# A phase seam in a fused adapter kernel: the last two layer norms finished on VectorE, and the first x of the next phase turned six pairs early

## The chip, the cores and the metric

The kernel runs on one core of a Trainium2 chip. Its engines are TensorE (PE in the profile, PEld for its weight loads), VectorE (DVE), ScalarE (ACT), GpSimd (POOL) and SyncE (SP, which here issues nearly all DMAs). The metric is the device time of one execution in microseconds, as the median of several executions. Before the change it is 3129.63 us (three runs, 3129.15 to 3130.18).

## The reference

The input x has 128 samples of 128 rows and 1024 columns (H), in float32. Each sample has a role from 0 to 2, which picks its weights. Two layers of the same form follow one another:

```python
def _L0_cond_ref(role, hidden_states, W_down, b_down, W_up, b_up, gamma, beta):
    h = jnp.einsum('bsh,bhk->bsk', hidden_states, W_down[role]) + b_down[role][:, None, :]
    h = jax.nn.gelu(h, approximate=False)
    u = jnp.einsum('bsk,bkh->bsh', h, W_up[role]) + b_up[role][:, None, :]
    y = hidden_states + u
    mean = jnp.mean(y, axis=-1, keepdims=True)
    var = jnp.mean(jnp.square(y - mean), axis=-1, keepdims=True)
    yn = (y - mean) * jax.lax.rsqrt(var + LN_EPS)
    return yn * gamma[role][:, None, :] + beta[role][:, None, :]
```

K, the width in between, is 512. The second layer takes the first one's output and its own weights.

## The kernel before

The work has four phases: down of layer 0, up of layer 0, down of layer 1, up of layer 1. Each phase goes over 64 items: 63 pairs of samples with the same role, and one pair of left-over samples (place 31 of the order). Pair n is item n in the first half and item n + 1 behind the left-overs, so the last two items of a phase are the pairs 61 and 62. Between the phases the data goes through DRAM: `hd` holds the hidden values, `mid` the output of layer 0.

A pair is one matrix product of 2 x 2 blocks done with seven block products instead of eight (the Winograd form). `item_products` gives them as steps s1 to s7 at the times 0, 2, 4 ... 12, and an item starts every 7 slots, so that the steps of two neighbouring items alternate on PE. The seven weight blocks have the names B11, B21, T2, T1, T3, B22, T4. They lie in `wall`, which has eight slots: seven for the phase at work and a spare one, into which the next phase's B11 is loaded early. Each block has three places, one for each role; the first 21 pairs of a phase use place 0 alone.

The seven products need sums of blocks of the transposed input. `Down.load` and `load_rest` bring x in eight quarter loads (L404), `turn` (L546) transposes one sample on VectorE, and `winograd_sums` (L413) makes four additions on POOL (L418 to L421). For the first three items of the second down phase there is no free buffer for x, so it goes into parts of weight blocks that aren't loaded yet (`among_weights`): item 0 into places 1 and 2 of B11, which lies in the slot that was spare.

In an up phase VectorE adds each product to x (L681, L690). At the end of a pair (`Up.finish`) each sample goes through: `squares` on ACT, ending in a power on POOL (L794); `scaled` on VectorE (L801); `stored`, for sample 0 a multiplication on ACT (L808) and an addition of beta on POOL (L809), for sample 1 one operation on VectorE (L811); `away`, the store to `mid` (L815).

What sets the order is a list of events with times in slots (`at`). The program runs through them in order of time and ties each instruction to the one before it on its engine. So every engine, and SP's queue of DMAs, works strictly in the order of the event times, however late it is. The loads of a phase's weight blocks (L937) and of the next x stand in the same SP queue as the stores of `away`. The event times of item 0 of phase 2, relative to its start, are: load -15, first turn with the rest of `prepare` -6.9, second turn and sums -3.5.

Of the kernel before, what the change touches and what calls it, by code (L numbers as in the profile page):

```python
# [14 lines left out]
ENG = mybir.EngineType  # L15
# [4 lines left out]
P = 128  # L20
SQ = 32
NQ = P // SQ
# [4 lines left out]
def kernel(  # L27
# [36 lines left out]
    ORDER = ["B11", "B21", "T2", "T1", "T3", "B22", "T4"]  # L64
# [8 lines left out]
    NI = NPAIR + 1  # L73
# [99 lines left out]
    class Sums:  # L173
# [23 lines left out]
        def load(self, q):  # L197
            if q == 0:
                self.role = reg(role_of, self.k, [ENG.SP], R - 1)
            rows = self.w.shape[1] // NQ  # L200
            src = self.w[ds(self.role, 1), ds(q * rows, rows), :]
            nc.sync.dma_start(self.whole[ts(q, SQ)], src.rearrange(self.rows, i=SQ))
# [196 lines left out]
    def quartered(t, srcs):  # L399

        for s, src in enumerate(srcs):
            n = src.shape[-1] // NQ
            for q in range(NQ):
                nc.sync.dma_start(  # L404
                    t[s][ts(q, SQ)], src[:, ts(q, n)].rearrange("(a t) c -> t a c", t=SQ)
                )
# [110 lines left out]
    class Down:  # L517
# [5 lines left out]
            self.tag = f"d{layer}_{n}"  # L523

        def load(self):
            if self.among_weights:


                block = self.ph.weights[ORDER[self.m]].v
                self.xq = [block[:, 1 + s] for s in range(2)]  # L530
            else:
                self.xq = [flat("q", 4, f"xq{self.tag}_{s}", H) for s in range(2)]
            self.xq = [t.rearrange("p (a c) -> p a c", a=NQ) for t in self.xq]
            if self.early:
                quartered(self.xq[0:1], [self.early_x(0, ENG.SP)])
                return
            self.srcs = x_of(self.layer, self.n, ENG.SP)
            quartered(self.xq[0:1], self.srcs[0:1])

        def load_rest(self):  # L540
            quartered(self.xq[1:2], [self.early_x(1, ENG.SP)] if self.early else self.srcs[1:2])

        def early_x(self, s, engine):
# [14 lines left out]
                self.turn(0)  # L558

        def prepare(self):  # L560
            self.begin_turns()
            self.sums = None
            set_places(self, [ENG.PE, ENG.Activation])
            if not self.early and self.n < NPAIR:
                self.sums = flat("s", 3, "S" + self.tag, 1792)[:, 0:1536].rearrange(
                    "p (m j c) -> p m j c", m=3, c=P
                )

        def end_turns(self):
            if self.early:  # L570
                return
            self.turn(1)
            if self.n < NPAIR:
                winograd_sums(self.sums, self.a, nc.vector if self.ph is phases[0] and self.m == 1 else nc.gpsimd)

# [47 lines left out]
    class Up:  # L623
# [150 lines left out]
        def finish(self):  # L774
            if self.last:
                return self.finish_last()
            steps = []
            for s in range(2):
                t = (10.4, 12.4)[s] if self.n < NPAIR else (10.9, 12.65)[s]
                one = lambda n: small.tile([P, 2], F32, tag=n, name=n + self.tag, bufs=6)  # L780
                box = {}
                row = lambda t, s=s: self.row(t, s)
                if self.before_last and s == 1:
                    before_last[:] = [self, box]

                def squares(s=s, box=box, one=one):
                    part, box["m"], box["v"] = one("part"), one("mean"), one("var")
                    nc.scalar.mul(part, self.stat[:, s], -1.0 / H)  # L788
                    m, v = box["m"][:, 0:1], box["v"][:, 0:1]
                    nc.scalar.activation(m, part[:, 0:1], AF.Identity, bias=part[:, 1:2])  # L790
                    box["o"] = flat("q", 4, f"o{self.tag}_{s}", H)
                    nc.scalar.activation(box["o"], self.x[:, s], AF.Square, bias=m, accum_out=v)  # L792
                    nc.scalar.activation(v, v, AF.Identity, bias=eps, scale=1.0 / H)  # L793
                    nc.gpsimd.tensor_tensor(v, v, mhalf[:, 0:1], ALU.pow)  # L794

                def scaled(s=s, box=box, row=row):
                    if self.before_last and s == 1:
                        nc.scalar.activation(box["o"], self.x[:, s], AF.Identity, bias=box["m"][:, 0:1])
                        nc.gpsimd.tensor_tensor(box["o"], box["o"], row(self.ph.gamma), ALU.mult)
                        return  # L800
                    nc.vector.scalar_tensor_tensor(  # L801
                        box["o"], self.x[:, s], box["m"][:, 0:1], row(self.ph.gamma), ALU.add, ALU.mult
                    )

                def stored(s=s, box=box, row=row):
                    o, v = box["o"], box["v"][:, 0:1]
                    if s == 0 and not self.before_last:
                        nc.scalar.mul(o, o, v)  # L808
                        nc.gpsimd.tensor_tensor(o, o, row(self.ph.beta), ALU.add)  # L809
                    else:  # L810
                        nc.vector.scalar_tensor_tensor(o, o, v, row(self.ph.beta), ALU.mult, ALU.add)  # L811

                def away(s=s, box=box):
                    if self.layer == 0:
                        nc.sync.dma_start(mid[self.n][s], box["o"])  # L815
                    else:
                        i = reg(perm, 2 * self.n + s, [ENG.SP], B - 1)
                        result(i, box["o"], slice(0, H), nc.sync)

                steps += [(t, squares), (t + 1.3, scaled)]  # L820


                if not (self.before_last and s == 1):
                    steps.append((t + (3.2 if self.before_last else 3.1), stored))
                    steps.append((t + (5.4, 4.2)[s], away))
            return steps
# [4 lines left out]
    SLOTS = 7  # L831
# [3 lines left out]
    def at(time, step):  # L835
        heapq.heappush(events, (time, next(count_), step))
# [7 lines left out]
    for k, ph in enumerate(phases):  # L844
        for m, n in enumerate(sequence):
            base = SLOTS * (k * NI + m)
            box = {}
            kind = Up if ph.up else Down

            def load(box=box, ph=ph, n=n, kind=kind, m=m):  # L850
                item = box["item"] = kind(ph, n)
                item.m = m
                item.early = ph is phases[0] and m == 0
                item.last = ph is phases[-1] and m == NI - 1
                item.before_last = ph is phases[-1] and m == NI - 2
                item.among_weights = ph is phases[2] and m < 3
                if m == left_over_at + 1:
                    item.SEED = -1.65
                item.load()


            if ph.up:
                first, rest = (-16 if m < 3 else -11.5), -7
            elif k == 0:
                first = {0: -30, 1: -19, 2: -19, 3: -17.4}.get(m, -19)
                rest = -28 if m == 0 else first + 0.05
            else:
                first = -15 if m == 0 else -11.9
                rest = first + 0.1
            at(base + first, load)  # L870
            at(base + rest, lambda box=box: box["item"].load_rest())

            def go(box=box, base=base):
                item = box["item"]
                item.prepare()
                if not item.among_weights:
                    item.end_turns()
                for time, step in item.products() + item.finish():
                    at(base + time, step)


            prepare = {1: 4.5 - base, 2: 8.6 - base}.get(m, kind.PREPARE) if k == 0 else kind.PREPARE
            if ph is phases[2] and m < 3:

                prepare = -6.9
                at(base - 3.5, lambda box=box: box["item"].end_turns())
            at(base + prepare, go)
        if k + 1 < len(phases):

# [43 lines left out]
            for name, (slot, free) in zip(ORDER, places):  # L933
                nxt.weights[name] = block = Block(slot)

                def load_part(k, to=block, src=scratch[nxt.layer, nxt.up][name]):
                    nc.sync.dma_start(to.v[:, k], src[:, k])  # L937


                at(base + free + 0.75, lambda f=load_part: f(0))  # L940
                for k_ in range(1, R):
                    later_on = SLOTS * (1 + 2 * ORDER.index(name) + k_)
                    at(base + later_on - 2.75, lambda f=load_part, k_=k_: f(k_))
    for i, job in enumerate(later):
        start = SLOTS * (7 + 6 * i)
# [72 lines left out]
```

## Time and profile before

| what | us |
|---|---|
| median of three runs | 3129.63 |
| the profiled execution | 3130.06 |
| its span, first to last instruction | 3128.3 |
| PE busy | 3112.7 |
| VectorE busy | 1975.8 |
| POOL busy | 1777.3 |
| ACT busy | 1203.5 |
| share of the 16 DMA engines (main queue) | 66.2% |

The page gives busy time by engine, the waits that ended last before an instruction, and a timeline in which each row has a start, a length, the engine, the line of the kernel and the tiles (out, then in). `xTd` is a transposed x, `Sd` the sums, `bd`, `ad` and `ed` are PSUM banks of a down item, `bu`, `au` and `eu` those of an up item, `ou` is an output on its way to the store, `varu` its variance. A row's bracket tells how long the engine stood before it and what released it. PE is busy in 99% of the span, with its clock at 0.999 of full speed on average. Around 1560.6 us the second down phase starts; this place is called the seam here.

### The profile page before, as it was taken

To read this page: it belongs to the slowest core of one execution; us is meant where nothing else is said; L and a number is where in the kernel's file an instruction comes from. 1 tells how busy PE (TensorE), PEld (TensorE's weight loads), DVE (VectorE), ACT (ScalarE), POOL (GpSimd) and SP (SyncE) were. 2 spreads that over 40 slices of the span, in tenths; PEclk is the share of its full clock that TensorE was granted. 3 is DMA by queue.
4 is the path that set the end of the run, shared out by engine and by line. 5 is a ranking of instruction groups with operands and counts; after the bars stand their busy time and mean duration, and the time that the engine had idled before them with its cause. 6 is when DMAs were issued, how large, how long until landed. Compare 5 with 4: busy or idle time off the path is not lost.

```text
span 3128.3 us, 42229 instructions
## 1 busy us (share of the span) xinstructions
PE 3112.7 (99%) x10796; PEld 2047.8 (65%) x10796; DVE 1975.8 (63%) x2807; ACT 1203.5 (38%) x2816; POOL 1777.3 (57%) x1391
## 2 busy tenths in 40 slices
PE   9999999999999999999999999999999999999999
PEld 6888888888544444444478888888884444444443
DVE  6554544544678777777864444444447877777777
ACT  1222222222454555454432222222224545454544
POOL 3545344444577767777654343444436777677775
PEclk9999999999999999999999999999999999999999
DMA  8778788876786565656687555555567765656564
GB/s 218 196 216 209 212 206 210 213 209 196 272 288 240 211 227 208 225 212 226 225 224 179 146 130 131 130 127 138 126 183 275 280 239 206 227 207 226 211 227 176
DMA packets 429735, 642.21 MB, mean 205 GB/s; under 512 B 35778, under 2 KB 305603, under 8 KB 428356
## 3 DMA queue, kind: packets, MB, share of 16 engines
q1 hardware_dynamic: 428930, 637.15, 66.2%
q8 instruction: 102, 1.67, 0.2%
q10 hardware_dynamic: 578, 2.36, 0.2%
q14 instruction: 125, 1.02, 0.1%
HBM read 405.02 MB, written 234.36 MB: 204 GB/s over the span
## 4 chain that ended last, share of the span: by engine, by line
PE 49%; POOL 1%; issue 0%; DMA 0%; SPq 0%; DVE 0%; ACT 0%; DVEq 0%; POOLq 0%; ACTq 0%
PE bu L427 14%; PE bd L427 14%; PE eu L427 7%; PE ed L427 7%; PE au L427 3%; PE ad L427 3%; POOL ou L809 0%; SPq L404 0%; DMA hd<-hd 0%; POOL Sd L420 0%; POOL Sd L418 0%; DMA wall<-mid 0%; POOL varu L794 0%; POOL xTd L419 0%; DVE ou L712 0%
## 5 line engine op out<-in xcount | busy, mean ns | idle before, releaser
L427 PE MATMUL bu<-wall,hTu 128*128 (+1 forms) x2048 | 921.3, 592 | 0.0
L547 DVE STREAM_TRANSPOSE xTd<-xqd 128x1024 f32<-128x1024 f32 (+1 forms) x252 | 504.9, 2071 | 350.7 <-PE bd L427 283.8
L427 PEld LDWEIGHTS bu<-wall,hTu 128*128 128x128 f32 x2048 | 389.1, 190 | 487.2 <-issue 456.6
L418 POOL TENSOR_TENSOR Sd<-xTd 128x512 f32<-128x512 f32 x124 | 159.7, 1288 | 790.4 <-DVE xTd L547 782.7
L794 POOL TENSOR_TENSOR varu<-varu,mhalf 128x1 f32<-128x1 f32 x254 | 329.6, 1298 | 393.8 <-ACT varu L793 393.8
L427 PE MATMUL bd<-wall,xTd 128*128 (+1 forms) x2064 | 487.1, 379 | 1.8 <-ACT bd L445 1.8
L427 PE MATMUL eu<-wall,hTu 128*128 (+1 forms) x1040 | 488.0, 592 | 0.0
L427 PE MATMUL bd<-wall,Sd 128*128 (+1 forms) x2000 | 472.8, 379 | 2.2 <-ACT hd L606 1.6
L427 PEld LDWEIGHTS bd<-wall,xTd 128*128 128x128 f32 x2064 | 392.0, 190 | 57.5 <-ACT bd L445 2.6
L427 PEld LDWEIGHTS bd<-wall,Sd 128*128 128x128 f32 x2000 | 379.7, 190 | 56.5 <-issue 2.6
L801 DVE SCALAR_TENSOR_TENSOR ou<-xu,meanu,tables 128x1024 f32<-128x1024 f32 x253 | 325.3, 1286 | 138.3 <-ACT ou L792 120.0
L611 ACT ACTIVATE hd<-hd 128x256 f32<-128x256 f32 x379 | 157.6, 416 | 534.5 <-DVE hd L610 534.4
L427 PEld LDWEIGHTS eu<-wall,hTu 128*128 128x128 f32 x1040 | 197.6, 190 | 247.4 <-issue 218.8
L788 ACT ACTIVATE partu<-statu 128x2 f32<-128x2 f32 x254 | 51.6, 203 | 728.7 <-DVE xu L690 728.7
L809 POOL TENSOR_TENSOR ou<-ou,tables 128x1024 f32<-128x1024 f32 x126 | 296.9, 2356 | 0.0
L792 ACT ACTIVATE ou<-xu,meanu 128x1024 f32<-128x1024 f32 x254 | 291.7, 1148 | 8.4
L681 DVE TENSOR_TENSOR xu<-bu,xu 128x512 f32<-128x512 f32 x256 | 176.1, 688 | 119.1 <-PE bu L427 119.1
L427 PE MATMUL ed<-wall,xTd 128*128 (+1 forms) x1064 | 251.0, 379 | 0.0
L418 POOL TENSOR_TENSOR hTu<-hTu 128x256 f32<-128x256 f32 x126 | 198.1, 1572 | 70.8 <-DVE hTu L656 49.0
L427 PE MATMUL au<-wall,hTu 128*128 (+1 forms) x504 | 236.8, 592 | 0.0
L427 PE MATMUL ed<-wall,Sd 128*128 (+1 forms) x1000 | 236.3, 379 | 0.1
L427 PE MATMUL ad<-wall,xTd 128*128 (+1 forms) x1000 | 236.2, 379 | 0.0
(135 smaller groups left out, 3383.1 us busy)
## 6 DMA issues: line engine op xcount, KB each, us to landing
xqd<-in_x_dram SPq DMA_DIRECT2D x512, 128.0 KB, 3.3
hd<-hd SPq DMA_DIRECT2D x256, 256.0 KB, 2.4
xu<-in_x_dram SPq DMA_DIRECT2D x128, 512.0 KB, 3.8
mid<-ou SPq DMA_DIRECT2D x128, 512.0 KB, 4.2
xu<-mid SPq DMA_DIRECT2D x128, 512.0 KB, 3.8
out_dram<-ou SPq DMA_DIRECT2D x125, 512.0 KB, 3.8
hqu<-hd SPq DMA_DIRECT2D x244, 256.0 KB, 5.0
xqd<-mid SPq DMA_DIRECT2D x488, 128.0 KB, 3.8
```

The costliest lines, as they stand in the source:

```text
L418: engine.tensor_tensor(dst[:, 1], a11, a21, ALU.subtract)
L427: nc.tensor.matmul(ps[:, 0:cols], a[:, j], w.rhs(r, j, cols), start=start and j == 0, stop=j == n - 1, skip_group_check=True,)
L547: nc.vector.transpose(self.a[:, s, chunks].rearrange("p j (t a) -> p j a t", t=SQ), self.xq[s].rearrange("p a (i j) -> p j a i", i=SQ)[:, ...
L611: nc.scalar.activation(y, y, AF.Gelu)
L681: nc.vector.tensor_tensor(y, ps, y, ALU.add)
L788: nc.scalar.mul(part, self.stat[:, s], -1.0 / H)
L792: nc.scalar.activation(box["o"], self.x[:, s], AF.Square, bias=m, accum_out=v)
L794: nc.gpsimd.tensor_tensor(v, v, mhalf[:, 0:1], ALU.pow)
L801: nc.vector.scalar_tensor_tensor(box["o"], self.x[:, s], box["m"][:, 0:1], row(self.ph.gamma), ALU.add, ALU.mult)
L809: nc.gpsimd.tensor_tensor(o, o, row(self.ph.beta), ALU.add)
```

## The change

Three things are changed.

- The last two pairs of the first up phase (`ending`) finish sample 0 as sample 1 is finished, in one operation on VectorE; both samples' last operation and store get earlier event times (2.5 and 3.6 behind the squares, in place of 3.1 and 4.2 or 5.4).
- Item 0 of the second down phase (`ahead`) gets its x much earlier. Both samples are loaded one after the other into place 0 of B11's block in the spare slot (events at -42 and -31.5), and turned (-34.8 and -24.3) into places 1 and 2 of the same block, from which PE reads them. The sums move from -3.5 to -8.4. Item 0 has no buffer of its own for the transposed x any more.
- Since B11's places 1 and 2 hold x until item 0 is done, the loads of places 1 and 2 for the second down phase change their turn: B21 comes first, B11 last.

```diff
         def load(self):
+            if self.ahead:
+                self.srcs = x_of(self.layer, self.n, ENG.SP)
+                self.a = self.ph.weights[ORDER[0]].v[:, 1:3].rearrange("p s (j c) -> p s j c", c=P)
+                return
             if self.among_weights:
...
+        def load_ahead(self, s):
+
+            self.xq = [self.ph.weights[ORDER[0]].v[:, 0].rearrange("p (a c) -> p a c", a=NQ)] * 2
+            quartered(self.xq[s : s + 1], self.srcs[s : s + 1])
+
         def load_rest(self):
+            if self.ahead:
+                return
             quartered(self.xq[1:2], [self.early_x(1, ENG.SP)] if self.early else self.srcs[1:2])
...
         def prepare(self):
-            self.begin_turns()
+            if not self.ahead:
+                self.begin_turns()
...
-            self.turn(1)
+            if not self.ahead:
+                self.turn(1)
...
+            ending = self.layer == 0 and self.m >= NI - 2
...
-                    if s == 0 and not self.before_last:
+                    if s == 0 and not self.before_last and not ending:
                         nc.scalar.mul(o, o, v)
                         nc.gpsimd.tensor_tensor(o, o, row(self.ph.beta), ALU.add)
                     else:
...
                 steps += [(t, squares), (t + 1.3, scaled)]
+                if ending:
+                    steps += [(t + 2.5, stored), (t + 3.6, away)]
+                    continue
...
+                item.ahead = ph is phases[2] and m == 0
...
+            elif m == 0:
+                first = rest = -43
+                for s in range(2):
+                    at(base - 42 + 10.5 * s, lambda box=box, s=s: box["item"].load_ahead(s))
+                    at(base - 34.8 + 10.5 * s, lambda box=box, s=s: box["item"].turn(s))
             else:
-                first = -15 if m == 0 else -11.9
+                first = -11.9
                 rest = first + 0.1
...
-                prepare = -6.9
-                at(base - 3.5, lambda box=box: box["item"].end_turns())
+                prepare = -6.9 if m else -8.5
+                at(base - 3.5 if m else base - 8.4, lambda box=box: box["item"].end_turns())
...
                 for k_ in range(1, R):
-                    later_on = SLOTS * (1 + 2 * ORDER.index(name) + k_)
+
+                    turn = ORDER.index(name) if nxt.up else (ORDER.index(name) - 1) % len(ORDER)
+                    later_on = SLOTS * (1 + 2 * turn + k_)
                     at(base + later_on - 2.75, lambda f=load_part, k_=k_: f(k_))
```

## The prediction

> **What bounds the kernel.** I read the page's busy table first, then the waits of PE, then busy time in slices of 10 us around the seam between the first up phase and the second down phase, then the timeline of that seam engine by engine, and last the slices in which PE's clock is not full.
>
> ```profile
> span 3128.3 us, 42229 instructions
> ...
> PE 3112.7 (99%) x10796; PEld 2047.8 (65%) x10796; DVE 1975.8 (63%) x2807; ACT 1203.5 (38%) x2816; POOL 1777.3 (57%) x1391
> ```
>
> PE is idle for 15.6 us in all. Nothing else bounds the kernel, so an edit is worth what it does to PE's waits. About 11.5 us of the idle time lie in the first 40 us and the last 12 us, which the change doesn't touch. The rest lies at the seam (columns: stretch, its length, then busy us of PE, PEld, DVE, ACT, POOL, PE clock, DMA share, GB/s):
>
> ```profile
> 1560.00:1570.00 10.00, 9.51 (x35) 6.22 (x34) 8.35 (x11) 4.83 (x11) 8.43 (x7) 1.00 0.94 321
> 1570.00:1580.00 10.00, 9.10 (x37) 6.45 (x35) 8.13 (x9) 5.03 (x14) 5.64 (x4) 1.00 0.79 209
> 1580.00:1590.00 10.00, 8.53 (x37) 6.77 (x37) 9.33 (x7) 4.04 (x11) 6.39 (x5) 1.00 0.55 197
> 1590.00:1600.00 10.00, 8.74 (x41) 7.38 (x41) 5.43 (x6) 2.35 (x7) 7.66 (x6) 1.00 1.06 291
> ```
>
> PE misses 0.49, 0.90, 1.47 and 1.26 us: 4.1. Ends of matmuls are modelled, so I count starts: from the product that starts at 1560.62 (first of the down phase) to the one at 1599.30 there are 19 steps in 38.68 us, at an even pace of 1.725 (the chain has 3.45 for two products) 32.78. **5.9 us are lost at the seam, and that is all the change can win: 0.19%.** The bound for a measured difference is 0.2%, 6.26 us.
>
> The first wait is for the weight block T2, and its queue tells why it is late:
>
> ```profile
> 1552.58 1.32 POOL L794 TENSOR_TENSOR varu<-varu,mhalf 128x1 f32<-128x1 f32 x1 [2.45 <-ACT varu L793]
> ...
> 1553.87 2.38 POOL L809 TENSOR_TENSOR ou<-ou,tables 128x1024 f32<-128x1024 f32 x1
> ...
> 1556.28 0.32 SPq L815 DMA_DIRECT2D mid<-ou  x1
> 1556.65 5.07 SPq L404 DMA_DIRECT2D wall<-mid  x8
> ...
> 1562.30 2.03 SPq L937 DMA_DIRECT2D wall<-T  x3
> ...
> 1568.16 1.97 PE L427 MATMUL bd<-wall,Sd 128*128 128x256 f32 x8 [0.49 <-DMA wall<-T]
> ```
>
> SP issues in order. It stood 5.4 us (waits of the queue) for POOL's beta addition of pair 60, sample 0 (ends 1556.27), then issued that store, eight quarters of x for item 1, another store, and only then T2: 6.02 us after POOL's end. PE got T2 5.86 us after its issue. PE wanted it at 1565.79 + 1.725 = 1567.52.
>
> **The change, part by part.**
>
> *The turns of item 0.* Two transposes leave the seam (2.0 us each: the row at 1554.01 is followed at 1556.02) and go into the up phase, one into each of the pairs that start some 57 and 45 us before the seam: the new order puts the first behind the addition at 1503.30, the second behind the one at 1521.93.
>
> ```profile
> 1503.30 0.69 DVE L681 TENSOR_TENSOR xu<-bu,xu 128x512 f32<-128x512 f32 x1
> ...
> 1521.93 0.68 DVE L690 SCALAR_TENSOR_TENSOR xu<-eu,xu 128x512 f32<-128x512 f32 x1
> ...
> 1533.90 0.68 DVE L690 SCALAR_TENSOR_TENSOR xu<-eu,xu 128x512 f32<-128x512 f32 x1
> ```
>
> The first runs 1503.91 to 1505.92; the addition behind it started at 1504.17: VectorE is 1.75 late. Does it catch up? From 1521.93 to 1533.90 VectorE and ACT, already late, need 11.97 for a pair, PE 12.01 (products at 1512.56 and 1524.57). So late stays late. The second turn adds 0.67: behind it VectorE waited 1.27 for ACT in any case (1521.93 + 0.62 + 2.01 + 0.61 = 1525.17, where the scaling started at 1524.50). Sum **+2.4 us** on all that follows in the up phase; bounds 0 (caught up) and 4.0 (both in full). PE feels a little of it: the third product of pair 59 is drained at 1526.3 + 0.7 = 1527.0 instead of 1523.2, and the next product on that bank was due at 1526.28: about 0.8, and 0.4 more in the next pair. I don't add these 1.2, since the wait below ends later whatever PE lost before.
>
> *Their eight x loads* go from 1534.8 (one batch of 4.7 us on SP) to two batches of four among pairs 56 to 58. SP issues 2.9 us per up pair there, so I cost them at nothing; if that cover were gone, a load of x for a pair would be 2.4 us late, against about 4 us it has in hand.
>
> *The sums of item 0 on POOL.* Four additions, in the new order behind the power of pair 60, sample 1, and **ahead of the beta addition of pair 60, sample 0**, on which SP waits. The power ended at 1553.90; with +2.4 it ends at 1556.3. The sums take 5.3 us undisturbed (1606.43 to 1611.74). They are disturbed: POOL and VectorE exclude one another on such operations.
>
> ```profile
> 1569.61 2.34 POOL L809 TENSOR_TENSOR ou<-ou,tables 128x1024 f32<-128x1024 f32 x1
> 1569.67 3.36 DVE L811 SCALAR_TENSOR_TENSOR ou<-ou,varu,tables 128x1024 f32<-128x1024 f32 x1 [0.34 <-POOL varu L794]
> ```
>
> The later starter stands until the other is done (1571.95) and then needs 1.08. Two VectorE operations (L811 of pair 60, L801 of pair 61) fall into the sums' time and cost POOL about 1.05 each: first sum to 1557.6, L811 to 1558.6, second sum 1559.8, third 1561.1, fourth 1562.5, L801 to 1563.5, and the beta addition (2.2 behind a collision) to **1565.8** where it was 1556.27. Bounds: 1561.7 (no lateness, no collision: 1553.9 + 5.4 + 2.4) and 1567.4 (4.0 late).
>
> *What is queued behind it.* On SP: the store, eight quarters of item 1, a store, T2, T1, T3, B22. T2 is issued 6.0 later, at 1571.8 (1570.9 if the batch takes 4.15, as at 1572.35), and lands 5.86 later by its own row, 3.65 at the least (B21 at 1550.52 on quiet engines, by its landing in the trace). I take 1571.4 + 5.6 = **1577.0** for PE's start; ends 1574.5 and 1579.2. On POOL: the power of pair 61, sample 0, for which VectorE's new L811 of that sample now waits (to 1566.4), and behind that the drain of pair 62's e bank, which PE needs at 1567: a new wait of 1 to 2 us on PE. It lies inside the wait for T2.
>
> *PE's clock.* PE then stands idle for some 7 us at once.
>
> ```profile
> 15.00:16.00 1.00, 0.98 (x2) 0.49 (x3) 1.00 (x2) 0.00 (x0) 0.00 (x0) 0.85 1.05 265
> 16.00:18.00 2.00, 2.00 (x4) 0.70 (x3) 1.97 (x2) 0.00 (x0) 0.00 (x0) 0.50 1.05 249
> ...
> 3122.50:3125.00 2.50, 0.16 (x1) 0.00 (x0) 1.42 (x2) 0.58 (x1) 0.00 (x0) 1.00 0.70 287
> 3125.00:3126.00 1.00, 0.00 (x0) 0.00 (x0) 0.00 (x0) 0.00 (x0) 0.00 (x0) 0.62 1.02 397
> ```
>
> The last column but two is the granted clock. It halves 2.6 us after PE's last matmul (3122.66, clock 0.62 over 3125 to 3126), and after the thin start of the kernel PE works at half clock from 15.7 to 19.1 (the stretch of 18 to 19 has 0.50 too, that of 19 to 20 has 0.94): 3.4 us that did 1.7 us of work. Waits of up to 1.5 us at the seam left it at 1.00. I add **1.75**; ends 0 (the clock stays) and 3.5 (twice that stretch). [...]
>
> *The end on VectorE.* For sample 0 of pairs 61 and 62 ACT's multiplication (1.13) and POOL's addition (2.35) go and VectorE gets L811 (1.27): 2.5 more on VectorE. In return both L811 of sample 1 lose their collision (3.36 to 1.27): 4.2 less, besides the two turns. The stores of 61 no longer wait on POOL for 7 us. So the five later waits (three for ACT, which stood behind VectorE; one for POOL's sums; one for an h buffer whose store was behind SP's wait) have less reason, and PE comes 9 us later to them. I cost them at nothing. The nearest is the h store: SP gets there at about 1595, it lands 5.2 later, and PE asks at 1591.7 + 11.3 = 1603.
>
> *The loads of places 1 and 2* of each block move by one turn (B21 first, B11 last): as many loads at the same times. Their first use is at pair 21, the last now lands at pair 13. Nothing.
>
> **Sum.** 1577.0 - 1567.5 = 9.5, refill 0.1, clock 1.75: 11.3 lost at the seam in place of 5.9: **+5.4 us**. On the profiled execution (3130.06, span plus 1.76) that is 3135.5; on the median 3129.63, which is 0.43 less, **3135.0**: +0.17%, within the bound.
>
> **Rivals.** *T2 later still (slower).* In the old run T2 left SP ahead of the crowd. Now T2, T1, T3, B22 and the next batch go out without a pause, and the old rows of T1 to B22 show 6.5 to 7.4 us to landing. With 7.4 behind 1571.8 PE starts at 1579.2: 11.7 + 0.1 + 1.75 - 5.9 = +7.6, 3137.2. It decides from a start at 1577.9. Against it: T2 is still the first of that crowd.
>
> *The waits go.* If the sums cost the store nothing (POOL stands idle 2.4 us before each power), only T2's own 0.7 stays of the 5.9: -5.2, 3124.4. For it: VectorE loses 4 us of work at the seam. Against it: the order on POOL is fixed, the sums behind that power and ahead of that addition.
>
> [...]
>
> **How the numbers follow.** Forecast 0.50 (+2 to +6.2), T2 later still or a longer half clock 0.33 (+6.3 to +9.5), waits gone 0.12 (-1 to -6), between 0.05. More than 6.26 to win doesn't exist at the seam, so faster by over 0.2% gets 0.02, slower 0.33, the rest within. The range 3128.5 to 3138.5 leaves out most of the "waits gone" case and the top of the slower one, some 2 in 10. The forecast's own range is 3131.6 to 3135.9.
>
> **What would show it.** Right: SP's store of pair 60, sample 0, at about 1566; T2 issued near 1571.5; one PE wait of 6 to 9 us on a wall<-T DMA; clock 0.5 for over 3 us behind it; almost no PE waits after that; VectorE 2.4 later at the additions of pairs 59 to 61. Wrong: that store before 1560, or PE waiting in several places again, or a T2 that lands within 4 us.

## The result, and the profile after

| | before | after |
|---|---|---|
| median, us | 3129.29 (22 runs, 3128.08 to 3131.95) | 3134.52 (22 runs, 3133.42 to 3136.34) |
| ratio | 1 | 1.0016, 95% interval 1.0010 to 1.0022 |
| the profiled execution | 3130.06 | 3135.67 |
| its span | 3128.3 | 3133.8 |

The change costs 5.2 us, 0.16%. The lines of the new kernel are numbered higher: the power is L809 (was L794), the operation `scaled` L816 (L801), POOL's addition of beta L824 (L809), VectorE's last operation L826 (L811), the store L830 (L815), the loads of the blocks L961 (L937), the drains of an up item L694 and L703 (L681, L690), and those of a down item L623 on VectorE and L619 on ACT (L610, L606). From the page of the new kernel:

```profile
span 3133.8 us, 42228 instructions
...
PE 3114.0 (99%) x10796; PEld 2049.4 (65%) x10796; DVE 1975.9 (63%) x2809; ACT 1202.2 (38%) x2814; POOL 1775.5 (57%) x1389
```

The span is 5.5 us longer, and every engine is busy as long as before to within 2 us, so the loss is again idle time of PE, or a slower clock. The waits of PE from 1500 to 1620 us (in all, times, longest) hold all of the first:

```profile
PE bd L427 <- DMA wall<-T: 6.2, 1, 6.2
PE eu L427 <- DVE xu L694: 1.0, 1, 1.0
PE bu L427 <- DVE xu L694: 0.7, 2, 0.5
```

In the kernel before, the same view has six short waits that sum to 4.1 us (ACT 3.4, T2 0.5, POOL's sums 0.2). The five others are gone, and the one for T2 has grown from 0.5 to 6.2 us. The timeline shows how it arises:

```profile
1554.73 1.33 POOL L809 TENSOR_TENSOR varu<-varu,mhalf 128x1 f32<-128x1 f32 x1 [2.44 <-ACT varu L808]
1556.03 1.27 POOL L418 TENSOR_TENSOR Sd<-wall 128x512 f32<-128x512 f32 x1
1557.37 2.13 POOL L419 TENSOR_TENSOR wall<-wall 128x512 f32<-128x512 f32 x1
1559.59 1.27 POOL L420 TENSOR_TENSOR Sd<-wall 128x512 f32<-128x512 f32 x1
1560.93 1.27 POOL L421 TENSOR_TENSOR Sd<-wall,Sd 128x512 f32<-128x512 f32 x1
1562.16 3.33 POOL L824 TENSOR_TENSOR ou<-ou,tables 128x1024 f32<-128x1024 f32 x1
...
1565.53 0.32 SPq L830 DMA_DIRECT2D mid<-ou  x1
1565.90 4.17 SPq L404 DMA_DIRECT2D wall<-mid  x8
...
1570.64 2.21 SPq L961 DMA_DIRECT2D wall<-T  x3
```

Each trace counts from its own first instruction. Products that the change doesn't reach stand 0.14 us earlier in the new one (one starts at 1440.32, in the old trace at 1440.46), so 0.14 is added where the two are compared. The power of pair 60, sample 1, ends 2.3 us later than before (1556.06, was 1553.90). Then come the four sums of item 0, and only then the addition that SP's store waits for: it ends at 1565.49, where it ended at 1556.27. T2 leaves SP at 1570.64 in place of 1562.30. PE gets it at 1576.24, and its clock is low by then (columns as in the prediction's windows; the last but two is the clock):

```profile
1572.00:1574.00 2.00, 0.00 (x0) 0.00 (x0) 2.00 (x2) 0.00 (x0) 0.00 (x0) 1.00 1.08 336
1574.00:1575.00 1.00, 0.00 (x0) 0.00 (x0) 1.00 (x2) 0.00 (x0) 0.00 (x0) 0.86 0.97 393
1575.00:1576.00 1.00, 0.00 (x0) 0.00 (x0) 1.00 (x4) 0.26 (x1) 0.00 (x0) 0.50 1.10 397
1576.00:1581.00 5.00, 4.76 (x10) 3.54 (x11) 3.52 (x4) 2.76 (x8) 2.39 (x2) 0.50 0.98 357
1581.00:1582.00 1.00, 1.00 (x3) 0.27 (x2) 0.00 (x0) 0.00 (x0) 0.92 (x2) 0.72 1.01 413
1582.00:1583.00 1.00, 1.00 (x5) 0.71 (x4) 0.42 (x1) 0.00 (x0) 0.92 (x2) 1.00 1.06 353
```

Half clock lasts 0.28 + 6 + 0.56 = 6.84 us, and PE works in 5.3 of them. Counted by the starts of products, against the even pace of 1.725:

```profile
1565.16 1.89 PE L427 MATMUL ad<-wall 128*128 128x256 f32 x8
1568.07 1.96 PE L427 MATMUL eu<-wall,hTu 128*128 x4 [1.02 <-DVE xu L694]
1576.24 3.75 PE L427 MATMUL bd<-wall,Sd 128*128 128x256 f32 x8 [6.21 <-DMA wall<-T]
1579.78 2.76 PE L427 MATMUL bu<-wall,hTu 128*128 x4
1582.38 1.89 PE L427 MATMUL ed<-wall 128*128 128x256 f32 x8
```

The steps between these starts lose 1.18 (wait for the e bank), 6.44 (wait for T2), 1.81 and 0.88 (half clock: 2.69). The two short waits of the up phase cost 1.24 us when counted in the same way: 39.00 us from the product at 1522.72 to the first of the down phase at 1561.72, where the kernel before has 37.76 (1522.86 to 1560.62). That is 11.55 us in all, against 5.9 before: +5.65. The two profiled executions differ by 5.61, the medians by 5.23.

### The profile page after: what moved, and what is told of

Same layout as the page of the kernel before. It is cut to its first block, busy times and chain, and to the rows that moved or that the text cites. A ratio compares the mean times of both kernels' runs of the same rounds, so it can differ in the third digit from the quotient of the medians.

```text
span 3133.8 us, 42228 instructions
## 1 busy us (share of the span) xinstructions
PE 3114.0 (99%) x10796; PEld 2049.4 (65%) x10796; DVE 1975.9 (63%) x2809; ACT 1202.2 (38%) x2814; POOL 1775.5 (57%) x1389
## 5 line engine op out<-in xcount | busy, mean ns | idle before, releaser
L809 POOL TENSOR_TENSOR varu<-varu,mhalf 128x1 f32<-128x1 f32 x254 | 331.7, 1306 | 395.2 <-ACT varu L808 395.1
L816 DVE SCALAR_TENSOR_TENSOR ou<-xu,meanu,tables 128x1024 f32<-128x1024 f32 x253 | 326.1, 1289 | 136.6 <-ACT ou L807 124.0
L824 POOL TENSOR_TENSOR ou<-ou,tables 128x1024 f32<-128x1024 f32 x124 | 293.4, 2366 | 0.0
L694 DVE TENSOR_TENSOR xu<-bu,xu 128x512 f32<-128x512 f32 x256 | 175.8, 687 | 118.5 <-PE bu L427 118.5
L418 POOL TENSOR_TENSOR hTu<-hTu 128x256 f32<-128x256 f32 x126 | 197.8, 1570 | 72.3 <-DVE hTu L669 60.4
```

The lines of the kernel that those rows point to most:

```text
L418: engine.tensor_tensor(dst[:, 1], a11, a21, ALU.subtract)
L694: nc.vector.tensor_tensor(y, ps, y, ALU.add)
L816: nc.vector.scalar_tensor_tensor(box["o"], self.x[:, s], box["m"][:, 0:1], row(self.ph.gamma), ALU.add, ALU.mult)
```

## The experiments

The theories on trial were these. **Q**: the order on POOL holds up the addition of beta, through it SP's store, and through SP's queue T2; PE's clock adds to it. **T**: the turns of item 0 make VectorE late, and that is the loss. **E**: the new ends of pairs 61 and 62 carry it. After the first runs two more were needed for the gain that did not come. **D**: drains (the operations that read a PSUM bank out, so that PE can fill it again) that stand behind the operations of the end on VectorE eat it. **W**: there is too much work at the seam in any order, and a wait only changes its place. All diffs are against the changed kernel where nothing else is said. The kernel before, timed beside these kernels, had medians of 3129.15 to 3129.32.

**sums_behind**: the sums go behind the addition of beta of pair 60.

```diff
-                at(base - 3.5 if m else base - 8.4, lambda box=box: box["item"].end_turns())
+                at(base - 3.5 if m else base - 7.45, lambda box=box: box["item"].end_turns())
```

> The changed kernel with one edit: the four sums of item 0 stand on POOL directly behind the beta addition of pair 60, sample 0, instead of ahead of it. Theory Q (queue): the addition ends about 1558.5 instead of 1565.5, the store of pair 60 follows at once, T2 is issued about 1563.5 to 1564.6 instead of 1570.6 and PE gets it about 1570; PE's wait for T2 falls from 6.2 us to 1.5 to 3, the clock stays at 1.00, and the time falls by 5 to 8 us against the changed kernel, to 3126 to 3130. Rival T (turns: the loss is VectorE's lateness from the two early turns, whatever POOL's order): the time stays within 2 us of 3134.5. Rival E (the new ends on VectorE cost it): the same, 3134.5.

Measured: 3129.18, ratio 0.9999 (0.9990 to 1.0008). The store leaves SP at 1557.89, T2 at 1563.20, and PE doesn't wait for T2 at all, where 1.5 to 3 us were expected:

```profile
1557.89 0.32 SPq L830 DMA_DIRECT2D mid<-ou  x1
...
1563.20 2.12 SPq L961 DMA_DIRECT2D wall<-T  x3
...
1569.35 1.89 PE L427 MATMUL bd<-wall,Sd 128*128 128x256 f32 x8
```

One event time takes the whole loss back, with turns and ends in place: Q stands; neither T nor E can be the main cause.

**store_behind**: POOL keeps its order, but the store of pair 60, sample 0, goes behind T2, T1 and T3 in SP's queue.

```diff
-                    steps.append((t + (5.4, 4.2)[s], away))
+                    late = self.layer == 0 and self.m == NI - 3
+                    steps.append((t + (10.4 if late else 5.4, 4.2)[s], away))
```

> The changed kernel with one edit: on SP the store of pair 60, sample 0, stands behind the loads of T2, T1 and T3 instead of ahead of the x loads of item 1. POOL's order and all compute are as in the changed kernel. Theory Q: SP no longer stands for POOL, T2 is issued before 1562 and PE doesn't wait for it; about 1 us (the e bank of pair 62) and 0.8 in the up phase stay, the clock stays at 1.00; 3125 to 3128. Rival T and rival E, and any theory in which POOL's or VectorE's lateness itself holds PE: PE still waits 4 us or more at item 0's third product and the time stays above 3131.

Measured: 3128.69, ratio 0.9999 (0.9990 to 1.0008). T2 leaves SP at 1559.97, 2.8 us earlier than in the kernel before (this trace runs 0.48 late), and PE doesn't wait for it. So the late addition does harm only by way of SP's queue. But the time lies above the 3125 to 3128 expected, and neither kernel beats the one before, though PE's old waits are gone. The waits of PE from 1560 to 1600 in sums_behind, and VectorE's timeline there:

```profile
PE bd L427 <- DVE hd L623: 1.4, 1, 1.4
PE bu L427 <- DVE xu L703: 1.2, 1, 1.2
PE eu L427 <- DVE xu L694: 1.0, 1, 1.0
```

```profile
1565.53 1.28 DVE L826 SCALAR_TENSOR_TENSOR ou<-ou,varu,tables 128x1024 f32<-128x1024 f32 x1 [1.06 <-POOL varu L809]
1566.73 0.68 DVE L694 TENSOR_TENSOR xu<-eu,xu 128x512 f32<-128x512 f32 x1
...
1570.49 1.25 DVE L826 SCALAR_TENSOR_TENSOR ou<-ou,varu,tables 128x1024 f32<-128x1024 f32 x1
1571.65 0.69 DVE L703 SCALAR_TENSOR_TENSOR xu<-bu,xu 128x512 f32<-128x512 f32 x1
...
1584.48 1.29 DVE L826 SCALAR_TENSOR_TENSOR ou<-ou,varu,tables 128x1024 f32<-128x1024 f32 x1 [1.02 <-POOL varu L809]
1585.69 0.42 DVE L623 TENSOR_TENSOR hd<-bd,hd 128x256 f32<-128x256 f32 x1
```

Each of the three drains that PE waits for stands right behind a last operation L826, and two of these had waited themselves for POOL's power. With the two short waits of the up phase that makes 4.3 us, as much as the old ones. This is where D came from.

**pe_filled**: 14 more products into a bank that isn't used at that time, ahead of item 0's third step. They add work and change no result; PE idles less than 0.1 us in front of T2.

```diff
+                if cols == K // 2 and item.layer == 1 and item.m == 0:
+                    fill = bank("a", item.tag + "_fill")
+                    for j in range(14):
+                        nc.tensor.matmul(
+                            fill[:, 0:cols], A(0, 0)[:, j % NQ], w["B11"].rhs(r, j % NQ, cols),
+                            start=j == 0, stop=j == 13, skip_group_check=True,
+                        )
```

> The changed kernel with 14 more matmuls of item 0's first operands, into a bank that nobody reads, ahead of item 0's third product: they take 6.0 us at full clock and lie in the wait for T2. If the clock is a cost of its own: T2 lands as before, the granted clock stays at 1.00 over 1574 to 1582, PE runs at full pace behind the wait, and the time falls by 2 to 3 us, to about 3132. If the clock's fall costs nothing: the time stays at 3134.5 or rises by what the filling overruns the wait.

Measured: 3132.15, ratio 1.0010 (1.0001 to 1.0019). T2 comes as late as in the changed kernel: it is issued at 1569.30, 8.91 us behind the start of the phase's first product, as there (8.92). But the clock stays at 1.00, over 1570 to 1580 and over 1580 to 1590.

```profile
1568.53 6.21 PE L474 MATMUL ad_fill<-wall 128*128 128x256 f32 x28
1574.82 1.97 PE L427 MATMUL bd<-wall,Sd 128*128 128x256 f32 x8
1576.62 1.88 PE L427 MATMUL bu<-wall,hTu 128*128 x4
1578.34 1.89 PE L427 MATMUL ed<-wall 128*128 128x256 f32 x8
```

The difference of the medians to the changed kernel, 2.4 us, is the clock's share. From the phase's first product (1560.39, there 1561.72) to the last of these rows (there 1582.38) the traces differ by 2.71, as much as the 2.69 counted above.

**end_only**: the kernel before with the new ends alone.

```diff
+            ending = self.layer == 0 and self.m >= NI - 2
...
-                    if s == 0 and not self.before_last:
+                    if s == 0 and not self.before_last and not ending:
...
+                if ending:
+                    steps += [(t + 2.5, stored), (t + 3.6, away)]
+                    continue
```

> The kernel before with only the new ends of the last two pairs (one VectorE operation for sample 0, earlier stores); item 0's x is loaded and turned as before. Theory Q: POOL's order up to the store of pair 60 is that of the kernel before, so PE's wait for T2 stays at about 0.5 us; VectorE loses two collisions of 2 us and SP two waits of 7 to 8 us, so of the 5.9 us lost at the seam 1 to 4 come back: 3125.5 to 3128.5. Rival E: VectorE's two more operations hold PE's drains; 3131 or more.

Measured: 3128.38, ratio 0.9997 (0.9988 to 1.0006): within the range expected, but no gain that can be told from none. Its waits of PE from 1500 to 1600:

```profile
PE bu L427 <- DVE xu L690: 1.8, 1, 1.8
PE bd L427 <- DVE hd L610: 1.4, 1, 1.4
PE bd L427 <- POOL Sd L420: 0.7, 1, 0.7
```

The old waits are traded for two of D's kind (the drain of the first stands behind a last operation of VectorE that had waited 0.9 us for POOL's power, the second is as long as the one in sums_behind) and one for the sums, at the product that waited for T2 before. The ends don't carry the loss, but they bring these waits along without item 0's change.

**ahead_only**: the changed kernel with the old ends.

```diff
-            ending = self.layer == 0 and self.m >= NI - 2
+            ending = False
```

> The changed kernel without the new ends: pairs 61 and 62 finish as before the change, item 0 stays ahead. Theory Q (the sums of item 0 on POOL stand ahead of the addition of beta of pair 60, and through SP's queue T2 comes late): that order is unchanged, the addition ends near 1565, T2 leaves SP near 1571, PE has one wait of 5.5 to 7.5 us for T2 with half clock behind it, 3133 to 3135.5. Theory E (the new ends carry the loss): 3128.5 to 3131, and no wait over 3 us. Theory D adds: PE's wait of 1.0 us for the e bank of pair 62 goes in this kernel, since no operation of VectorE waits for POOL ahead of that drain; the wait for T2 is longer by as much.

Measured: 3134.83, ratio 1.0019 (1.0009 to 1.0028). The waits of PE from 1500 to 1620 are

```profile
PE bd L427 <- DMA wall<-T: 7.7, 1, 7.7
PE bu L427 <- DVE xu L694: 0.7, 2, 0.5
```

The loss is all there without the new ends: E falls. The wait for the e bank is gone, as D said, and that for T2 is longer instead: 7.7 (5.5 to 7.5 expected) against 6.2 + 1.0.

**no_turns**: the two transposes of item 0 are left out.

```diff
-                    at(base - 34.8 + 10.5 * s, lambda box=box, s=s: box["item"].turn(s))
```

> The changed kernel with the two transposes of item 0 left out (item 0 of the second down phase then works on what lies in the buffer; no other instruction goes). Theory Q with the lateness of VectorE as a term of its own (2.15 us by the power of pair 60): the waits of 0.5 and 0.2 us in the up phase go, the addition of beta of pair 60 ends near 1563.3 in place of 1565.5, T2 leaves SP near 1568.5 and PE starts on it near 1574.1; PE idles 4 to 5 us at that place, and the clock falls late or not at all. Time 3134.52 - 2.15 less up to 2.6 of clock: 3129.7 to 3132.4, ratio 1.0000 to 1.0010. If the lateness is no part of the loss (VectorE catches up, or the sums set the time alone): 3134 to 3135.

Measured: 3132.07, ratio 1.0008 (0.9999 to 1.0017). PE starts on T2 at 1574.51. This trace runs 0.53 us later than that of the changed kernel (the product at 1440.32 there starts at 1440.85 here), so that is 2.26 us earlier than with the turns (2.15 expected). The two waits of the up phase are gone. PE still idled 6.27 us, not the 4 to 5 expected, and the clock did fall (0.50 from 1573 to 1579): my expectation had left out that PE gets to T2 earlier too when the wait for the e bank goes (it started the step before at 1566.29, not 1568.07). The lateness is a real term of some 2 us; over half of the loss, 2.9 us against the kernel before, stays without it.

**ahead_store_behind**: store_behind with `ending = False`.

> The changed kernel without the new ends and with the store of pair 60, sample 0, behind the loads of T2, T1 and T3. Theory D: PE doesn't wait for T2, and of the waits of store_behind those of 1.0 (e bank) and 1.2 us (b bank) go, since their drains stand ahead of VectorE's operation again; the one of 1.4 us for the hidden values stays, since that operation stands where it stood, with perhaps 1 us more where VectorE and POOL collide: 3126.5 to 3127.8, ratio 0.9991 to 0.9994. Theory W: POOL's addition and ACT's multiplication bring the waits for ACT and POOL of the kernel before back (3 us or more), 3128.5 to 3130.

Measured: 3127.76, ratio 0.9994 (0.9984 to 1.0003). PE's waits for VectorE of 1.0 and 1.2 us are gone, as D said. The third is gone too, which it had not said; two waits for ACT (1.0 and 0.9) are there in its place, less than W's 3 us. They stand at the same two products where the kernel before had waited 1.3 and 1.2 us for ACT, so W is right in part: two of the old waits are back.

**late_end**: store_behind, with the last operations of pairs 61 and 62 behind those drains.

```diff
-                    steps += [(t + 2.5, stored), (t + 3.6, away)]
+                    steps += [(t + 4.2, stored), (t + 4.2 + 1.1, away)]
```

> The changed kernel with the store of pair 60, sample 0, behind the loads of T2, T1 and T3 (as in store_behind, 3128.69), and the last operation and the store of pairs 61 and 62 at 4.2 and 5.3 slots behind the squares in place of 2.5 and 3.6: VectorE then drains the e bank of pair 62, the first b bank after the seam and the hidden values of item 0 ahead of the operations that wait for POOL's powers. Theory D (the gain of the removed waits is eaten by drains that stand behind VectorE operations of the end): PE's waits of 1.0, 1.2 and 1.4 us at the seam go, the two of the up phase (0.5 and 0.2) stay, so 3128.69 - 3.6 = 3125.1, ratio to before 0.9986 (0.998 to 0.9993). Rival theory W (VectorE has too much work at the seam in any order, and the wait comes back at another place): one or more new waits that sum to 2.5 us or more, 3128 to 3130, ratio 0.9995 to 1.0003.

Measured: 3127.00, ratio 0.9990 (0.9981 to 1.0000): between D's 3125.1 and W's 3128. Its waits of PE from 1500 to 1620:

```profile
PE bd L427 <- DVE hd L623: 0.8, 1, 0.8
PE bu L427 <- DVE xu L694: 0.7, 2, 0.5
PE bd L427 <- ACT hd L619: 0.7, 1, 0.7
PE bu L427 <- DVE xu L703: 0.3, 1, 0.3
```

The e bank is free in time, two drains still stand behind an L826, and a wait for ACT is back, at the product where the kernel before had 1.3: ACT waits 6.7 us for a buffer of hidden values whose store stands in SP's queue behind a store of pair 62. W was partly right, but each of these has a place in an order, so the next kernel moved them further.

**later_end**: late_end with 5.2 and 7.2 in place of 4.2 and 5.3.

> late_end with the last operation of pairs 61 and 62 at 5.2 and their stores at 7.2 slots behind the squares (4.2 and 5.3 there). The b bank of pair 62 and the hidden values of item 0 are then drained ahead of the operations of the end, and SP issues the stores of item 0's hidden values ahead of pair 62's last store. Theory D (each wait left in late_end stands behind an operation of the end, on VectorE or in SP's queue): of its waits of 0.7 (up phase), 0.34 (b bank), 0.78 (hidden values) and 0.70 us (ACT behind a store of hidden values) the last three go, PE's idle time at the seam falls from 2.5 to 0.7 us, the time from 3127.0 to 3125.2, ratio to before 0.9987 (0.9978 to 0.9996). Theory W (another wait comes in their place): 1.5 us or more of new waits, 3126.7 to 3128.5.

Measured: 3125.32 (11 runs, 3124.93 to 3126.41), ratio 0.9988 (0.9979 to 0.9997): 4.0 us less than the kernel before, 9.2 less than the changed one. Its page and its waits of PE:

```profile
span 3123.6 us, 42228 instructions
...
PE 3111.4 (100%) x10796; PEld 2047.5 (66%) x10796; DVE 1974.8 (63%) x2809; ACT 1201.6 (38%) x2814; POOL 1774.2 (57%) x1389
```

```profile
PE bu L427 <- DVE xu L694: 0.7, 2, 0.5
PE bd L427 <- DVE hd L623: 0.4, 1, 0.4
```

Of the three waits that were to go, two are gone. The one for the hidden values is down from 0.8 to 0.4: its drain (1581.96) now stands behind a transpose and a scaling (L816) that took 2.38 us, in late_end 1.55. VectorE and ACT do the same work as in the changed kernel. Only the order differs, and PE's waits sum to 1.1 us in place of 7.9.

## Why the prediction was right, and where it was not

Forecast 3135.0, measured 3134.52; the way was the one described. By its steps:

- **PE bounds, and the seam is all there is.** Right: PE's waits and its clock between 1526 and 1583 give +5.65 us, where the profiled executions differ by 5.61.
- **The turns.** Lateness 2.4 forecast, 2.3 by the power of pair 60, sample 1; it was not caught up, and no_turns gets 2.26 of it back at T2. In the up phase PE waited 0.5 and 0.2 us and lost 1.24 by the starts of products, as forecast (0.8 and 0.4). By the event times the first load goes six pairs ahead of the phase, the turns five and three and a half.
- **The sums ahead of the addition.** From the end of that power to the end of the addition 9.5 us forecast, 9.43 measured, though the collisions fell elsewhere: one in the sums (the second, 2.13 in place of 1.27), and a larger one in the addition itself (3.33, in sums_behind 2.35). The end is 1565.63 on the old trace's count, forecast 1565.8.
- **SP's queue.** T2 went out at 1570.78 on the old trace's count (1571.4 forecast), PE had it 5.60 later (5.6 forecast). The start at 1576.38 is 0.6 earlier than forecast. That this queue is the path, sums_behind and store_behind show in two independent ways.
- **The wait for the e bank.** 1.0 of the forecast 1 to 2, and inside the wait for T2, as said: without it (ahead_only) PE waits 1.5 longer for T2.
- **The clock was mis-sized.** I took 1.75, one stretch of 3.4 us at half clock, from the row of the kernel's start. It was 6.84 us, twice as long, of which PE missed only the first 1.5 us and worked 5.3: 2.69 by the starts, 2.4 by pe_filled. Both lie within the ends of 0 and 3.5 that I gave. The clock also fell later than in the other row that I went by: 4.7 us behind the last matmul, where the kernel's end has 2.6.
- **The later waits at nothing.** Right in the changed kernel, where PE came to them later, behind T2. sums_behind brings PE there on time: the old waits are gone there too, but besides that for the e bank (1.0) there are two that the prediction had not seen (1.2 and 1.4 us), for drains behind the new ends. So the rival "the waits go" had the wrong price: with T2 on time the change was worth 0, not -5.2.
- **The loads of places 1 and 2.** No wait for them shows.

The sum: 9.6 for the waits forecast (PE's lateness ahead of T2 is in it), 1.24 + 1.18 + 6.44 = 8.9 measured; 1.75 for the clock, 2.7 measured. Two errors of 0.7 and 0.9 us with opposite signs left a total of 11.3 against 11.55; that the forecast lies within 0.5 us is in part luck.

## What to carry to other kernels

Work moved off the critical place is not free on the engine it moves to: look at what it is put ahead of on that engine's queue, and at which DMA queue waits for that. Here the order of five additions on POOL decided when PE got a weight block, 20 us later, by way of a store in SP's queue. An operation that has time (a last multiply and its store) belongs behind the drains that PE waits for, however early its inputs are ready: moved there in two steps, it took the time from 3128.69 us (store_behind) to 3125.32 (later_end). One long wait of PE cost its length and then 2.4 to 2.7 us of clock here; the short waits of the kernel before, up to 1.3 us each, left the clock at 1.00 in every stretch of 10 us from 1560 to 1600.

## What the runs showed of the hardware that was not expected

Half clock lasted 6.84 us or more, where the kernel's start has one stretch of 3.4. Three kernels idled PE for long at the seam:

| kernel | last matmul ends | half clock from, to | length | PE starts |
|---|---|---|---|---|
| after | 1570.03 | 1574.72, 1581.56 | 6.84 | 1576.24 |
| no_turns | 1568.24 | 1572.42, 1579.26 | 6.84 | 1574.51 |
| ahead_only | 1567.68 | 1570.04, 1580.28 | 10.24 | 1575.36 |

The times come from the mean clocks of 1 us windows at both ends, read as a mix of 1.00 and 0.50; in no_turns (two rows) and ahead_only (two rows):

```profile
1572.00:1573.00 1.00, 0.00 (x0) 0.00 (x0) 1.00 (x1) 0.00 (x0) 0.00 (x0) 0.71 1.02 406
...
1579.00:1580.00 1.00, 1.00 (x4) 0.50 (x3) 0.00 (x0) 0.00 (x0) 0.92 (x2) 0.87 1.03 422
```

```profile
1570.00:1571.00 1.00, 0.00 (x0) 0.00 (x0) 0.17 (x1) 0.00 (x0) 0.00 (x0) 0.52 1.14 219
...
1580.00:1581.00 1.00, 1.00 (x3) 0.41 (x3) 0.00 (x0) 0.00 (x0) 0.92 (x2) 0.86 1.11 234
```

The clock fell 2.4 to 4.7 us after the last matmul and rose 4.8 to 5.3 us after work began. The longer wait did not cost more of the clock: ahead_only waited 7.7 us for T2 and then worked 4.9 us at half clock, the changed kernel 6.2 and 5.3. What decides when the clock falls and when it rises was not tested by itself: these are three kernels, with modelled ends of matmuls.
